# Convolution matrices read in four row groups without their zero columns, and another order of the first loads

## The chip, the cores and the metric

The kernel runs on one core of one Trainium2 chip. The metric is the device time of one execution in microseconds (us), lower is better. Four runs of the kernel before gave 3228.2 to 3229.64 us, with a median of 3228.65.

## The reference

Two layers work on `x` of shape (32, 384, 28, 28) in float32: a ConvNeXt block, and a channel gate on its output. Cut to what matters:

```
# layer 0
y = depthwise 7x7 convolution of x (padding 3) + dw_b
y = layer norm of y over the 384 channels, times ln_g, plus ln_b
y = gelu(y @ w1 + b1)                       # 384 -> 1536
y = grn_g * (y * nx) + grn_b + y            # nx: norm over positions / mean of the norms
x = x + (y @ w2 + b2)                       # 1536 -> 384
# layer 1
avg, max, min of x over positions -> small products (W1, W2_1, W2_2, W3, Wfc) -> logits
out = sigmoid(logits[:, :, None, None] + x)
```

## The kernel before

The kernel has two stages: first the depthwise convolution of all 32 images, then, image by image, norm, first product, gelu, second product and gate. The change is in the first stage and in the loads ahead of it.

**The convolution as matrix products.** An image of 28 by 28 is cut into seven strips of four rows, and each row is padded to 32 columns, so a strip of one channel is 128 values: one partition each. For each channel, the 49 weights become a banded matrix that takes a strip to a strip. Three products per channel (L309, L310, L313) take a strip to itself and to its two neighbours, with 224, 192 and 192 columns (strips times images).

The matrices of one channel are one table row. `tab` (128 channels by 3 blocks by 448 columns) is cleared, the 49 weights are copied into it with a row distance of 32 (L183), and the three blocks are stored to `fs` in DRAM (L187). `load_t(s)` reads from `fs` the matrices of the eight channels of step `s` into `tmat[s % 3]`: the same row is read by each of the 128 partitions, one element later in each, so that the shifted copies form the matrix. One read covers 128 partitions by 8 channels by `MW` = 320 columns; most of the columns at the edges of the row are zeros from the cleared table. The first 32 columns of each `tmat` buffer are cleared once by POOL (L195).

**The turned x.** The products need x with strip positions on the partitions. `load_x(i)` (L227) reads 32 channels of four images as a tile `xi` (four buffers), `pad_x(i)` (L237, POOL) copies it into one of two `xpad` buffers with 32 columns per row, and `turn_x` (L248, L253) transposes the seven strips on TensorE and copies them from PSUM into `xt` by VectorE. Eight groups make one block of 32 channels, `xt`; there are 12 blocks.

**The loop.** 48 steps of eight channels: each issues `load_t(s + 2)`, does the 24 products, evacuates them with the bias `dwb` by ScalarE (L327) or VectorE (L319) into `yc`, and between the products pads and turns one group of the next block per four channels. Every second step stores `yc` to `yd` (L345). From step 4 on each step also has POOL form one combination of blocks of `w1s` or `w2s` (`form_w`, L270 and L272) and store it; 15 of each. These feed the second stage, which is a scheme with fewer products than the plain one.

**The order.** Tile's scheduler sets the order of the instructions of each engine and inserts the waits: it goes by the order in the program, but may let an instruction whose inputs it takes for ready pass others of its engine. On one engine, and on SP, which issues nearly all of the DMAs, instructions then run strictly in that order, so one that waits holds all behind it. The loads ahead of the loop stand in the program as:

```
nc.sync.dma_start(dww, ...); nc.sync.dma_start(cv, ...)      # L150, L154
... tab cleared and filled, fs stored; dwb loaded (L197)
for s in range(2): load_t(s)
for i in range(4): load_x(i)
nc.sync.dma_start(w1s, ...)                                  # L279
for i in range(NG): pad_x(i); load_x(i + 4); turn_x(i, 0..1)
nc.sync.dma_start(w2s, ...); nc.sync.dma_start(fv, ...)      # L287, L288
```

`cv` holds per-channel vectors for the second stage, `fv` those of the 1536 middle channels.

Of the kernel before, what the change touches and what calls it, by code (L numbers as in the profile page):

```python
# [13 lines left out]
P = 128  # L14
C = 384
CB = C // P
# [15 lines left out]
PW = P // RW  # L32
XC = 32
TC = 8
YC = 16
NB = P // XC
REACH = 3 * PW
MW = P + 2 * REACH
FL = MW + P
NLAST = XC // YC  # L40


# [71 lines left out]
def convnext_gate_kernel(  # L114
# [13 lines left out]
    nc = tc.nc  # L128
# [11 lines left out]

    fs = [dram.tile([P, FL], F32, name=f"fs_{cb}") for cb in range(CB)]
    NY = C // YC
    yd = dram.tile([P, NY - NLAST, B, NJ * YC], F32, name="yd")
    u1d = dram.tile([KT, P, NS, P], F32, name="u1d")
    u2d = dram.tile([NS, P, KT * P], F32, name="u2d")
    yl = dram.tile([P, NLAST, B, NJ * YC], F32, name="yl")


    dww = const.tile([P, CB, 49], F32, name="dww")
# [1 line left out]
    ident = const.tile([P, P], F32, name="ident")  # L151
    make_identity(nc, ident)
    cv = const.tile([P, 5, CB], F32, name="cv")
    nc.sync.dma_start(cv, cvec.rearrange("v (cb p) -> p v cb", p=P))  # L154
    _, lng_t, lnb_t, b2_t, w21_t = (cv[:, i, :] for i in range(5))
    fv = const.tile([P, 3, FB], F32, name="fv")
    b1_t, gg_t, gb_t = (fv[:, i, :] for i in range(3))
# [9 lines left out]
    with ExitStack() as one:  # L167
# [8 lines left out]
        w1s = tp.tile([P, CB, FF], F32, name="w1s")  # L176
        w2s = tp.tile([P, FB, C], F32, name="w2s")
        tab = tp.tile([P, CB, FL], F32, name="tab")
        nc.vector.memset(tab, 0.0)

        t0 = REACH + P - 1 - 3 * PW - 3
        for cb in range(CB):
            nc.vector.tensor_copy(  # L183
                tab[:, cb, t0 : t0 + 7 * PW].rearrange("p (y x) -> p y x", x=PW)[:, :, :7],
                dww[:, cb, :].rearrange("p (y x) -> p y x", x=7),
            )
            nc.sync.dma_start(fs[cb], tab[:, cb, :])  # L187

        NT2 = 3
        T0 = P - REACH
        tmat = [tp.tile([P, TC, T0 + MW], F32, name=f"tmat_{i}") for i in range(NT2)]
        for t in tmat:
            nc.gpsimd.memset(t[:, :, :T0], 0.0)  # L195
        dwb = tp.tile([P, C], F32, name="dwb")
        nc.sync.dma_start(dwb, cvec[0:1, :].broadcast_to([P, C]))  # L197
        NK = C // TC

        def load_t(s):  # L200
            base = fs[s * TC // P]
            c0 = s * TC % P
            nc.sync.dma_start(
                tmat[s % NT2][:, :, T0:],
                bass.AP(
                    tensor=base.tensor,
                    offset=base.offset + c0 * FL,
                    ap=[[1, P], [FL, TC], [1, MW]],
                ),
            )  # L210


        NPAD = 2
# [4 lines left out]
        NG = B // NB  # L218
# [3 lines left out]
        def load_x(i):  # L222

            k, g = divmod(i, NG)
            t = xis[i] = xip.tile([P, NT], F32, tag="xi", name=f"xi_{i}")
            base = x[g * NB, k * XC : k * XC + 1, :]
            nc.sync.dma_start(  # L227
                t,
                bass.AP(
                    tensor=base.tensor,  # L230
                    offset=base.offset,
                    ap=[[NT, XC], [C * NT, NB], [1, NT]],
                ),
            )

        def pad_x(i):
            nc.gpsimd.tensor_copy(  # L237
                xpad[i % NPAD][:, :, :HW], xis.pop(i).rearrange("p (r w) -> p r w", w=HW)
            )
# [18 lines left out]
        def new_xt(k):  # L258
            return xtp.tile([P, XC, N], F32, tag="xt", name=f"xt_{k}")
# [12 lines left out]
                    nc.gpsimd.tensor_tensor(t, t, blk, ALU.add if sg > 0 else ALU.subtract)  # L272
            nc.sync.dma_start(dst, t)

        for s in range(2):
            load_t(s)
        for i in range(4):
            load_x(i)
        nc.sync.dma_start(w1s, w1.rearrange("(cb p) f -> p cb f", p=P))  # L279
        xt = new_xt(0)  # L280
        for i in range(NG):
            pad_x(i)
            if i + 4 < GT:
                load_x(i + 4)
            for h in range(2):
                turn_x(i, h, xt)
        nc.sync.dma_start(w2s, w2.rearrange("(fb p) c -> p fb c", p=P))  # L287
        nc.sync.dma_start(fv, fvec.rearrange("v (fb p) -> p v fb", p=P))  # L288
        SK = XC // TC
        GS = NG // SK  # L290
        for s in range(NK):
            k, si = divmod(s, SK)
            if s + 2 < NK:
                load_t(s + 2)
            if si == 0:
                xn = new_xt(k + 1) if k + 1 < NX else None
            if s % 2 == 0:
                kt = s // 2
                yc = ycp.tile([P, B, NJ, YC], F32, tag="yc", name=f"yc_{kt}")
            if s == NK - 2:  # L300
                warm = smp.tile([P, 1], F32, tag="warm", name="warm", bufs=1)
                nc.scalar.activation(warm, eps_t, AF.Sqrt)
            t = tmat[s % NT2]
            for c2 in range(TC // 2):
                pc = psc.tile([P, 2, 256], F32, tag="pc", name=f"pc_{s}_{c2}")
                for ci in range(2):
                    c = 2 * c2 + ci
                    xc = xt[:, si * TC + c, :]
                    nc.tensor.matmul(pc[:, ci, :N], t[:, c, P : 2 * P], xc, start=True, stop=False)  # L309
                    nc.tensor.matmul(  # L310
                        pc[:REACH, ci, : N - B], t[:, c, 2 * P :], xc[:, B:], start=False, stop=False
                    )
                    nc.tensor.matmul(  # L313
                        pc[:, ci, B:N], t[:, c, :P], xc[:, : N - B], start=False, stop=True
                    )
                cc = s * TC + 2 * c2
                cy = cc % YC
                if c2 % 2:
                    nc.vector.tensor_tensor(  # L319
                        yc[:, :, :, cy : cy + 2].rearrange("p b j c -> p c j b"),  # L320
                        pc[:, :, :N].rearrange("p c (j b) -> p c j b", j=NJ),
                        dwb[:, cc : cc + 2].unsqueeze(2).unsqueeze(3).to_broadcast([P, 2, NJ, B]),
                        ALU.add,
                    )
                else:
                    for ci in range(2):
                        nc.scalar.activation(  # L327
                            yc[:, :, :, cy + ci].rearrange("p b j -> p j b"),
                            pc[:, ci, :N].rearrange("p (j b) -> p j b", j=NJ),
                            AF.Identity,  # L330
                            bias=dwb[:, cc + ci : cc + ci + 1],
                            scale=1.0,
                        )
                if xn is not None:
                    g, h = divmod(si * (TC // 2) + c2, 2)
                    i = (k + 1) * NG + g
                    if h == 0:
                        pad_x(i)
                        if i + 4 < GT:
                            load_x(i + 4)  # L340
                    turn_x(i, h, xn)
            if s % 2:
                yv = yc.rearrange("p b j c -> p b (j c)")
                if kt < NY - NLAST:
                    nc.sync.dma_start(yd[:, kt], yv)  # L345
                else:
                    i = kt - (NY - NLAST)
                    for j in range(NJ):
                        nc.vector.bn_stats(bs0[:, j, 1 + i, :], yc[:, 0, j, :])
                    nc.vector.tensor_copy(yis[0][:, kt], yc[:, 0])  # L350
                    nc.sync.dma_start(yl[:, i], yv)
                if kt == NY - NLAST - 1:

                    yi = yis[0] = yip.tile([P, NY, NJ, YC], F32, tag="yi", name="yi_0")
                    nc.sync.dma_start(
                        yi[:, : NY - NLAST].rearrange("p k j c -> p k (j c)"), yd[:, :, 0, :]
                    )
                    bs0 = smp.tile([P, NJ, 1 + NLAST, 6], F32, tag="bs0", name="bs0", bufs=1)
                    for j in range(NJ):
                        nc.vector.bn_stats(bs0[:, j, 0, :], yi[:, : NY - NLAST, j, :])  # L360
            if si == SK - 1:
                xt = xn
            i = s // 2 - 2
            if 0 <= i < NS:
                if s % 2 == 0:
                    form_w(f"u1_{i}", w1v, UPSTEPS[i][1], u1d[:, :, i, :].rearrange("t p c -> p t c"))
                else:
                    form_w(
                        f"u2_{i}", w2v, STEPS[i][1], u2d[i].rearrange("p (t c) -> p t c", c=P)
                    )  # L370
# [470 lines left out]
```

## Time and profile before

| | |
|---|---|
| median of 4 runs | 3228.65 us |
| profiled execution, own time | 3230.04 us |
| its span (first to last instruction) | 3228.2 us |
| TensorE (PE) busy | 3177.5 us, 98% |
| first convolution product | 37.33 us from the start |
| last matrix load issued | 485.1 us |
| DMA traffic | 534.10 MB, mean 165 GB/s |

The profile is of one execution. Engines: PE is TensorE's products, PEld its weight loads, DVE VectorE, ACT ScalarE, POOL GpSimd, and SPq the queue of SyncE, which issues DMAs. L203 is line 203 of the kernel before. A timeline row gives the start and the length in us, the engine, the line, the operation, what it writes and reads, shapes and count, and in brackets the idle time of the engine ahead of it with what ended it. A row of waits gives the total in us, the number of times and the longest. "x" after a number in a row of stretches is the count of instructions; the last columns are TensorE's granted clock, the mean busy share of the 16 DMA engines, and GB/s.

### The profile page before, as it was taken

The numbers are of one execution on the slowest core, as the hardware profiler recorded it, in microseconds if no ns is written. First come the engines' busy times: TensorE is split into PE (matmuls) and PEld (weight loads), VectorE is DVE, ScalarE is ACT, GpSimd is POOL, SyncE is SP. The second block draws the span as 40 slices with busy tenths as digits, with TensorE's granted clock in tenths as the row PEclk, the third lists the DMA queues.
The fourth block names the chain that finished last, engine by engine and source line by source line (L and its number), as shares of the span: only waits on it lengthen the run. The fifth ranks groups of instructions, "written<-read, shape, count | busy, mean of one in ns | idle before, by whom it ended". The sixth has DMA issues, their size and how long they took to land.

```text
span 3228.2 us, 35684 instructions
## 1 busy us (share of the span) xinstructions
PE 3177.5 (98%) x12352; PEld 2012.4 (62%) x12352; DVE 1676.2 (52%) x3447; ACT 1882.0 (58%) x3024; POOL 1604.8 (50%) x813
## 2 busy tenths in 40 slices
PE   7999998999999999999999999999999999999998
PEld 6999996555555555555555555555555555555555
DVE  3443336555555555555555555555555555555553
ACT  1222224866666666666666666666666666666662
POOL 2455311555555555555555555555555555555555
PEclk9999999999999999999999999999999999999999
DMA  9999986434444444444444444444444444444333
GB/s 305 339 334 331 315 285 213 129 112 142 141 142 139 135 132 140 142 132 142 145 134 143 145 134 144 134 143 145 145 131 137 131 134 143 140 142 141 123 104 125
DMA packets 300150, 534.10 MB, mean 165 GB/s; under 512 B 121004, under 2 KB 179908, under 8 KB 296900
## 3 DMA queue, kind: packets, MB, share of 16 engines
q1 hardware_dynamic: 287572, 494.51, 47.1%
q10 hardware_dynamic: 12400, 37.33, 3.4%
q8 instruction: 98, 1.61, 0.2%
q14 instruction: 80, 0.66, 0.1%
HBM read 440.65 MB, written 91.13 MB: 165 GB/s over the span
## 4 chain that ended last, share of the span: by engine, by line
PE 87%; ACT 1%; DVE 1%; issue 0%; ACTq 0%; DVEq 0%
PE ph_A L549 13%; PE ph_B L549 13%; PE pz_A L646 11%; PE pz_B L646 10%; PE pz_C L646 5%; PE pz_E L646 5%; PE ph_C L549 5%; PE pz_F L646 3%; PE pz_G L646 3%; PE pz_D L646 3%; PE ph_H L549 3%; PE ph_D L549 3%; PE ph_F L549 3%; PE py L475 2%; PE pc L309 2%; PE pc L310 1%
## 5 line engine op out<-in xcount | busy, mean ns | idle before, releaser
L621 POOL TENSOR_TENSOR d_v<-d_u,y 128x1568 f32<-128x1568 f32 x32 | 112.4, 3511 | 759.6 <-PE pz_B L646 735.5
L524 ACT ACTIVATE y<-y,fv 128x784 f32<-128x784 f32 x384 | 346.8, 941 | 214.6 <-DVE y L564 214.0
L457 ACT ACTIVATE y<-y,fv,gsc 128x784 f32<-128x784 f32 x378 | 358.6, 1027 | 29.8 <-DVE gsc L591 29.8
L327 ACT ACTIVATE yc<-pc,dwb 128x224 f32<-128x224 f32 x192 | 103.7, 641 | 402.8 <-PE pc L313 303.5
L530 ACT ACTIVATE junk<-y 128x784 f32<-128x784 f32 x384 | 326.7, 851 | 5.0
L621 POOL TENSOR_TENSOR d_p<-y 128x1568 f32<-128x1568 f32 x31 | 109.0, 3518 | 434.6 <-ACT y L457 434.6
L549 PE MATMUL ph_A<-af,u 128*128 128x392 f32 x768 | 313.4, 502 | 5.5 <-DVE af L515 5.4
L549 PE MATMUL ph_B<-af,u 128*128 128x392 f32 x768 | 311.3, 493 | 0.3 <-ACT y L556 0.3
L646 PE MATMUL pz_A<-y,u 128*128 128x392 f32 x768 | 268.8, 493 | 0.0
L621 POOL TENSOR_TENSOR y<-d_v,y 128x1568 f32<-128x1568 f32 x64 | 223.5, 3513 | 2.5
L549 PEld LDWEIGHTS ph_A<-af,u 128*128 128x128 f32 x768 | 136.1, 190 | 135.1 <-ACT y L556 57.6
L549 PE MATMUL ph_A<-acc,u 128*128 128x392 f32 x512 | 216.3, 504 | 0.0
L309 PE MATMUL pc<-xt,tmat 128*128 128x224 f32 x768 | 209.3, 354 | 4.9 <-issue 4.9
L549 PE MATMUL ph_B<-acc,u 128*128 128x392 f32 x512 | 213.6, 499 | 0.1
L549 PEld LDWEIGHTS ph_B<-af,u 128*128 128x128 f32 x768 | 145.1, 190 | 108.9 <-DVE y L560 9.6
L646 PEld LDWEIGHTS pz_A<-y,u 128*128 128x128 f32 x768 | 145.8, 190 | 106.4
L556 ACT ACTIVATE y<-ph_A 128x392 f32<-128x392 f32 x256 | 124.7, 487 | 144.9 <-PE ph_A L549 144.8
L560 DVE TENSOR_TENSOR y<-y,ph_A 128x392 f32<-128x392 f32 x128 | 72.0, 562 | 237.9 <-PE ph_A L549 224.6
L446 ACT ACTIVATE sd<-mv,eps_t 128x7 f32<-128x7 f32 x32 | 9.6, 300 | 314.3 <-DVE mv L441 314.3
L515 POOL TENSOR_TENSOR af<-af,acc 128x392 f32<-128x392 f32 x186 | 186.9, 1017 | 4.9
L310 PE MATMUL pc<-xt,tmat 128*96 128x192 f32 x768 | 187.6, 326 | 0.0
L313 PE MATMUL pc<-xt,tmat 128*128 128x192 f32 x768 | 187.6, 326 | 0.0
(153 smaller groups left out, 6907.1 us busy)
## 6 DMA issues: line engine op xcount, KB each, us to landing
u<-u1d SPq DMA_DIRECT2D x128, 960.0 KB, 4.6
u<-u2d SPq DMA_DIRECT2D x480, 256.0 KB, 2.7
tmat<-fs SPq DMA_DIRECT2D x48, 1280.0 KB, 7.8
yd<-yc SPq DMA_DIRECT2D x22, 1792.0 KB, 11.3
yi<-yd SPq DMA_DIRECT2D x32, 1232.0 KB, 6.9
xi<-in_x SPq DMA_DIRECT2D x96, 392.0 KB, 8.5
x<-in_x SPq DMA_DIRECT2D x32, 1176.0 KB, 5.8
out<-x ACTq DMA_DIRECT2D x31, 1176.0 KB, 5.0
```

Source lines behind the costliest of these rows:

```text
L309: nc.tensor.matmul(pc[:, ci, :N], t[:, c, P : 2 * P], xc, start=True, stop=False)
L310: nc.tensor.matmul(pc[:REACH, ci, : N - B], t[:, c, 2 * P :], xc[:, B:], start=False, stop=False)
L313: nc.tensor.matmul(pc[:, ci, B:N], t[:, c, :P], xc[:, : N - B], start=False, stop=True)
L327: nc.scalar.activation(yc[:, :, :, cy + ci].rearrange("p b j -> p j b"), pc[:, ci, :N].rearrange("p (j b) -> p j b", j=NJ), AF.Identity, b ...
L457: eng.activation(out, in_, AF.Identity, bias=add, scale=mul)
L515: eng.tensor_tensor(d, o[in0], o[in1], op)
L524: nc.scalar.activation(y, y, AF.Gelu, bias=b1_t[:, f : f + 1], scale=1.0)
L530: nc.scalar.activation(junk, ys[b][:, f, :], AF.Square, accum_out=ssqs[b][:, f : f + 1])
L549: nc.tensor.matmul(banks[bk][:, :NH], wt[:, i, :], o[opnd], start=(first == 1), stop=True, skip_group_check=True,)
L556: nc.scalar.activation(d, p, AF.Identity)
L621: nc.gpsimd.tensor_tensor(d, o[in0], o[in1], op)
L646: nc.tensor.matmul(pz[:, :NH], wt[:, t, :], o[opnd][:, t, :], start=(first == 1 and t == 0), stop=(t == KT - 1), skip_group_check=True,)
```

## The change

1. `load_t` reads each buffer in four DMAs of 32 partitions (`GR` = 32) instead of one of 128. Group `g` (0, 32, 64, 96) leaves out columns that are zero in all its 32 partitions: it reads 227, 230, 230 and 227 columns for the four groups, instead of 320.
2. The three `tmat` buffers are cleared whole on VectorE, instead of 32 columns of each on POOL; the first of them between the clearing of `tab` and the copies into it, the others after these.
3. The stores of `fs` are issued on ScalarE's queue instead of SP's.
4. The first four x loads stand ahead of `load_t(0)`; `dwb` and `load_t(1)` come at the fifth pad.
5. `w1s`, `w2s`, `fv` and `cv` are loaded at steps 2, 3, 4 and 5 of the loop. Ahead of each load, POOL copies one column of `yc` into the tile that is to be loaded, so the load waits for a product of the loop.

```diff
+S0 = REACH + P - 1 - 3 * PW - 3
+S1 = S0 + 6 * PW + 7
+GR = 32
...
-    nc.sync.dma_start(cv, cvec.rearrange("v (cb p) -> p v cb", p=P))
...
-        nc.vector.memset(tab, 0.0)
-        t0 = REACH + P - 1 - 3 * PW - 3
-        for cb in range(CB):
-            nc.vector.tensor_copy(tab[:, cb, t0 : ...], dww[:, cb, :]...)
-            nc.sync.dma_start(fs[cb], tab[:, cb, :])
...
-        for t in tmat:
-            nc.gpsimd.memset(t[:, :, :T0], 0.0)
         dwb = tp.tile([P, C], F32, name="dwb")
-        nc.sync.dma_start(dwb, cvec[0:1, :].broadcast_to([P, C]))
+        nc.vector.memset(tab, 0.0)
+        nc.vector.memset(tmat[0], 0.0)
+        for cb in range(CB):
+            nc.vector.tensor_copy(tab[:, cb, S0 : ...], dww[:, cb, :]...)
+            nc.scalar.dma_start(fs[cb], tab[:, cb, :])
+        for t in tmat[1:]:
+            nc.vector.memset(t, 0.0)
...
         def load_t(s):
             base = fs[s * TC // P]
             c0 = s * TC % P
-            nc.sync.dma_start(
-                tmat[s % NT2][:, :, T0:],
-                bass.AP(tensor=base.tensor, offset=base.offset + c0 * FL,
-                        ap=[[1, P], [FL, TC], [1, MW]]),
-            )
+            for g in range(0, P, GR):
+                m0, m1 = max(0, S0 - g - GR + 1), min(MW, S1 - g)
+                nc.sync.dma_start(
+                    tmat[s % NT2][g : g + GR, :, T0 + m0 : T0 + m1],
+                    bass.AP(tensor=base.tensor, offset=base.offset + c0 * FL + g + m0,
+                            ap=[[1, GR], [FL, TC], [1, m1 - m0]]),
+                )
...
-        for s in range(2):
-            load_t(s)
         for i in range(4):
             load_x(i)
-        nc.sync.dma_start(w1s, ...)
+        load_t(0)
         xt = new_xt(0)
         for i in range(NG):
             pad_x(i)
+            if i == NG - 4:
+                nc.sync.dma_start(dwb, cvec[0:1, :].broadcast_to([P, C]))
+                load_t(1)
             if i + 4 < GT:
                 load_x(i + 4)
             for h in range(2):
                 turn_x(i, h, xt)
-        nc.sync.dma_start(w2s, ...)
-        nc.sync.dma_start(fv, ...)
+        later = {2: (w1s, ...), 3: (w2s, ...), 4: (fv, ...), 5: (cv, ...)}
...
             if s + 2 < NK:
                 load_t(s + 2)
+            if s in later:
+                dst, src = later[s]
+                nc.gpsimd.tensor_copy(dst[:, 0, :1], yc[:, 0, 0, :1])
+                nc.sync.dma_start(dst, src)
```

More of the change, by code (lines that the diff above doesn't have):

```diff
@@ L178, in convnext_gate_kernel @@
         tab = tp.tile([P, CB, FL], F32, name="tab")
-        nc.vector.memset(tab, 0.0)
-        t0 = REACH + P - 1 - 3 * PW - 3
-        for cb in range(CB):
-            nc.vector.tensor_copy(
-                tab[:, cb, t0 : t0 + 7 * PW].rearrange("p (y x) -> p y x", x=PW)[:, :, :7],
-                dww[:, cb, :].rearrange("p (y x) -> p y x", x=7),
-            )
-            nc.sync.dma_start(fs[cb], tab[:, cb, :])
         NT2 = 3
@@ L193, in convnext_gate_kernel @@
         tmat = [tp.tile([P, TC, T0 + MW], F32, name=f"tmat_{i}") for i in range(NT2)]
-        for t in tmat:
-            nc.gpsimd.memset(t[:, :, :T0], 0.0)
         dwb = tp.tile([P, C], F32, name="dwb")
-        nc.sync.dma_start(dwb, cvec[0:1, :].broadcast_to([P, C]))
+        nc.vector.memset(tab, 0.0)
+        nc.vector.memset(tmat[0], 0.0)
+        for cb in range(CB):
+            nc.vector.tensor_copy(
+                tab[:, cb, S0 : S0 + 7 * PW].rearrange("p (y x) -> p y x", x=PW)[:, :, :7],
+                dww[:, cb, :].rearrange("p (y x) -> p y x", x=7),
+            )
+            nc.scalar.dma_start(fs[cb], tab[:, cb, :])
+        for t in tmat[1:]:
+            nc.vector.memset(t, 0.0)
         NK = C // TC
@@ L202, in load_t @@
             c0 = s * TC % P
-            nc.sync.dma_start(
-                tmat[s % NT2][:, :, T0:],
[L205 to L210, printed above, removed]
+            for g in range(0, P, GR):
+                m0, m1 = max(0, S0 - g - GR + 1), min(MW, S1 - g)
+                nc.sync.dma_start(
+                    tmat[s % NT2][g : g + GR, :, T0 + m0 : T0 + m1],
+                    bass.AP(
+                        tensor=base.tensor,
+                        offset=base.offset + c0 * FL + g + m0,
+                        ap=[[1, GR], [FL, TC], [1, m1 - m0]],
+                    ),
+                )
         NPAD = 2
@@ L273, in form_w @@
             nc.sync.dma_start(dst, t)
-        for s in range(2):
-            load_t(s)
         for i in range(4):
             load_x(i)
-        nc.sync.dma_start(w1s, w1.rearrange("(cb p) f -> p cb f", p=P))
+        load_t(0)
         xt = new_xt(0)
@@ L286, in convnext_gate_kernel @@
                 turn_x(i, h, xt)
-        nc.sync.dma_start(w2s, w2.rearrange("(fb p) c -> p fb c", p=P))
-        nc.sync.dma_start(fv, fvec.rearrange("v (fb p) -> p v fb", p=P))
+        later = {
+            2: (w1s, w1.rearrange("(cb p) f -> p cb f", p=P)),
+            3: (w2s, w2.rearrange("(fb p) c -> p fb c", p=P)),
+            4: (fv, fvec.rearrange("v (fb p) -> p v fb", p=P)),
+            5: (cv, cvec.rearrange("v (cb p) -> p v cb", p=P)),
+        }
         SK = XC // TC
```

## The prediction

> **What bounds the kernel now.** I read the busy shares first, then the start in stretches of 2 us and as a timeline, then what TensorE waited for during the convolution, then stretches of 20 us, then the DMA issues. The page says who is the bound:
>
> ```profile
> PE 3177.5 (98%) x12352; PEld 2012.4 (62%) x12352; DVE 1676.2 (52%) x3447; ACT 1882.0 (58%) x3024; POOL 1604.8 (50%) x813
> ```
>
> TensorE is idle for 50.7 us of 3228.2 in all. The change touches only the start and the convolution (0 to 510 us), so its gain is capped by the idle time there. The timeline of the start:
>
> ```profile
> 8.03 0.84 POOL L237 COPY xpad<-xi 128x784 f32<-128x784 f32 x1 [5.53 <-DMA xi<-in_x]
> 8.62 1.00 SPq L203 DMA_DIRECT2D tmat<-fs  x2
> 9.66 4.43 SPq L227 DMA_DIRECT2D xi<-in_x  x2
> ...
> 21.55 0.84 POOL L237 COPY xpad<-xi 128x784 f32<-128x784 f32 x1 [10.02 <-DMA xi<-in_x]
> ...
> 28.16 1.49 POOL L270 TENSOR_SCALAR u<-w1s 128x512 f32<-128x512 f32 x1 [4.76 <-DMA w1s<-in_w]
> ...
> 30.49 6.93 PE L248 MATMUL pt<-ident,xpad 128*128 128x128 f32 x35 [4.79 <-POOL xpad L237]
> ...
> 37.33 0.65 PE L309 MATMUL pc<-xt,tmat 128*128 128x224 f32 x2
> ```
>
> The first product starts at 37.33. It needs eight x loads, padded by POOL and turned by TensorE. Loads 2 and 3 stand behind two matrix loads on SP, so POOL waits 10.02 us. Then POOL waits for w1s, since a product with w1s (written at step 4) was ordered ahead of pads 4 to 7. TensorE does 63 turns (nine groups of seven, one of them of the next block) in 13.7 us, so it is idle for 23.6 us before 37.33. This is the stall that the change can reach. During the convolution TensorE waits for little (waits of PE, 37 to 512 us):
>
> ```profile
> PE pc L309 <- issue: 4.9, 11, 1.1
> PE pt L248 <- POOL xpad L237: 1.9, 2, 1.5
> PE pt L248 <- DVE xt L253: 0.4, 1, 0.4
> ```
>
> But the DMA engines are as full as TensorE (columns: PE, PEld, DVE, ACT, POOL busy, clock, DMA share, GB/s):
>
> ```profile
> 4.00:6.00 2.00, 0.00 (x0) 0.00 (x0) 0.00 (x0) 0.00 (x0) 0.00 (x0) 1.00 0.94 114
> 6.00:8.00 2.00, 0.00 (x0) 0.00 (x0) 0.00 (x0) 0.00 (x0) 0.00 (x0) 1.00 0.98 375
> ...
> 100.00:120.00 20.00, 19.62 (x126) 18.87 (x125) 8.44 (x13) 4.17 (x8) 7.08 (x8) 1.00 0.99 344
> ...
> 340.00:360.00 20.00, 18.09 (x115) 17.11 (x115) 8.29 (x13) 3.23 (x6) 11.67 (x11) 1.00 0.94 318
> ```
>
> ```profile
> u<-u2d SPq DMA_DIRECT2D x480, 256.0 KB, 2.7
> tmat<-fs SPq DMA_DIRECT2D x48, 1280.0 KB, 7.8
> ...
> w1s<-in_w SPq DMA_DIRECT2D x1, 2304.0 KB, 13.9
> ```
>
> **The change part by part.** *The head of SP's queue.* cv leaves it (0.48 us of issue, and 1920 items of 4 bytes, beside which the engines were 94% busy at 114 GB/s between 4 and 6 us), dwb moves behind x, and the three fs stores go to ACT's queue, where nothing waits behind them. x0 to x3 are then issued from about 1.3 us at 0.55 each, instead of at 2.83, 5.18, 9.66 and 13.49. x0 took 5.2 us to its pad beside cv and dwb, so it lands by 6.5, and 0.40 MB at the 375 GB/s of the next row is 1.07 us more for each: x3 by 9.7.
>
> *VectorE.* The table's memset (1344 columns, 1.18 us) is followed by one of 2816 columns, 2.47 us at the same rate, ahead of the three copies (0.42 us). They end at 1.14 + 1.18 + 2.47 + 0.42 = 5.2 instead of 3.4. The first fs store goes out at about 4.95 and lands 5.0 us later (its own row): 9.95. Two further memsets of 2.47 us keep VectorE until 10.1, and behind them wait the copies of turned x, whose first came at 10.07 before; three PSUM buffers hold TensorE up after a group and a half. x4 covers this, landing later than 15; without that cover it would cost 2 to 3 us. POOL loses 0.81 us of memsets: nothing.
>
> *Load 0.* Four issues of 0.37 to 0.58 us instead of one: 10.0 to 11.8. A whole load landed after 6.2 us at the least: 16.2. x4 to x7 are issued behind it (their slots are free once pads 0 to 3 are through, by about 11) and stream at 1.07 us each: x7 at 20.5. From the start of a pad to the second copy's end the first group took 3.3 us (8.03 to 11.27). **First product at 23.8**, I take 24.0. If x4 to x7 get ahead of load 0, it is 20.5; if fs lands 4 us later, 28. Shift 13.3 us. One group of seven turns (1.5 us) that was done ahead of 37.33 will stand inside the convolution: **11.8 us** net. With the pads back to back, TensorE's own eight groups would have allowed 17 to 18; the DMA engines are what is late next.
>
> *w1s, w2s, fv, cv at steps 2 to 5.* 4.7 MB, and 6528 items of 4 bytes, now go beside the convolution; before, only w2s and fv did. Each waits on SP for a small POOL copy, which waits for ScalarE's first output of a pair of steps. Behind the copy on POOL are pads; behind the load on SP are x and matrix loads. The copy itself is one column (the smallest POOL row is 0.10 us). Before, POOL stood 9.0 us for w2s and SP 10.38 us in one matrix load's issue right behind fv, and TensorE lost 1.9 us to xpad. Two big loads at that price are about 4 us; w1s comes where little else is due, so I take 2.5. Bounds 0 and 12: two waits of 9.0 us less one pad period of 4.9 us that the second xpad buffer covers give 8.2, and 4 more for two stalls of SP.
>
> *The clock.* It read 0.50 between 30 and 36 us, after TensorE's idle 25.7 to 30.5, and fell on turns. TensorE will now idle from about 14 to 17. Should half clock reach the first products, 6.8 us of it cost at most 3.4. I take 0.5.
>
> *The matrices.* The groups read 227, 230, 230 and 227 columns instead of 320: 0.936 MB for 1.311 MB, but the same 1024 rows. In 1280 KB per load, 392 per x, 1792 per yd and 256 per form, two steps moved 6.59 MB in 19.7 us, 334 GB/s, and will move 5.84 MB, 297 GB/s. TensorE sets the pace of these steps, so fewer bytes bring nothing there by themselves; the 4.9 us of "issue" stay (bounds: minus 4.9 to 0). SP gets 144 more issues, 1.1 to 1.5 us per step of 9.85, in which it now spends some 2.5 us issuing. The price of a load split by rows is in no row of the trace. At 340 GB/s one load takes 3.86 us; by bytes the new one takes 2.75, by rows the same 3.86, and four unoverlapped transfers of 256 KB (2.7 us each to landing) would be 10.8. I take 2.75 to 3.86, since landings overlap everywhere in this trace (48 loads of 7.8 us fit among the others), and so no cost: the DMA share of about 0.97 leaves 0.6 us per two steps.
>
> [...]
>
> **Sum.** -11.8 + 2.5 + 0.5 = -8.8. The profiled execution took 3230.04 us (span 3228.2 and 1.84 around it), 1.4 above the median of 3228.65. So 3221.2 for a profiled one, **3219.9 for the median**. With the bounds of the start (20.5 to 28) and the usual part of the stalls, this case runs from 3214 to 3224.
>
> **The rivals.** *The DMA engines become the bound (slower).* For it: the share near 1 in every stretch up to 360 us, and row counts that do not fall. Against it: 29% fewer bytes. It decides once a load takes over 3.86 + 0.3 = 4.2 us; above, each us costs two per pair of steps, 24 pairs. At 5.0 us: (2 x 1.14 - 0.6) x 24 = 40 us, less 8.8: 3260; at 4.5 us it is 3234.
>
> *The late weights take the place of the stall (no change).* POOL stands for w1s and w2s with pads behind, 12 us as bounded: 11.8 gained and 12 to 13 lost, about 3229. For it: forms were put ahead of pads twice before (4.8 and 9.0 us). Against it: only 1.9 us reached TensorE.
>
> *It does not do what it says.* The instruction order is made by a scheduler with its own clock; if it puts load 0 or 1, with its wait for fs, ahead of most x loads, the first product comes at about 32: 5.3 - 1.5 = 3.8 us, less some stall, 3226.
>
> **How the numbers follow.** Main case 0.60, DMA bound 0.15, late weights 0.17, order 0.08. About 0.2% (6.5 us) is what a measurement can tell from no change. Faster by more: 0.58 of the main case and 0.04 from the milder ends of the next two, 0.62. Slower by more: 0.14 of the DMA case and 0.03 of the late weights, 0.17. Same: 0.21. The range 3213 to 3236 takes in the main case, both cases of no change and the mild end of the DMA case; some 0.15 stays out.
>
> **What would show it.** Right: first product between 20 and 28 us; POOL's 10.02 us wait and the w1s wait before it gone; DMA share in the 100 to 360 us stretches near 0.85 with about 297 GB/s; waits of PE on xpad within a few us. Wrong: a DMA share still near 1 at below 300 GB/s with waits of the products on tmat (DMA bound); POOL forms waiting 8 us or more for w1s or w2s and TensorE for xpad (late weights); matrix loads ahead of x2 to x5 on SP (order). A longer stretch after the convolution would be outside all of this.

## The result and the profile after

| | before | after |
|---|---|---|
| median | 3229.35 us (46 runs) | 3237.32 us (28 runs, 3233.14 to 3242.25) |
| ratio | 1 | 1.0024 [1.0019, 1.0029] |
| profiled execution, own time / span | 3230.04 / 3228.2 us | 3234.73 / 3232.7 us |
| first product | 37.33 us | 26.68 us |
| first product to the end of the last one of the convolution | 472.42 us | 488.10 us |
| from there to the end | 2718.5 us | 2717.9 us |

The change makes the kernel 8 us slower. The profiled execution of after is one of the quicker ones, 2.6 us under its median. Its three stretches say where to look: the start gained 10.65 us, the convolution lost 15.7, and behind it next to nothing changed (0.5 us). TensorE still carries the span:

```profile
PE 3180.1 (98%) x12352; PEld 2018.1 (62%) x12352; DVE 1680.0 (52%) x3450; ACT 1881.7 (58%) x3024; POOL 1606.4 (50%) x814
```

The start, from the timeline of after:

```profile
5.22 0.84 POOL L240 COPY xpad<-xi 128x784 f32<-128x784 f32 x1 [3.47 <-DMA xi<-in_x]
5.35 1.84 ACTq L196 DMA_DIRECT2D fs<-tab  x3
...
11.02 1.81 SPq L206 DMA_DIRECT2D tmat<-fs  x4
...
12.94 2.48 SPq L230 DMA_DIRECT2D xi<-in_x  x4
...
19.02 0.84 POOL L240 COPY xpad<-xi 128x784 f32<-128x784 f32 x1 [5.14 <-DMA xi<-in_x]
...
26.68 0.64 PE L323 MATMUL pc<-xt,tmat 128*128 128x224 f32 x2 [0.92 <-DVE xt L256]
```

The first pad comes at 5.22 instead of 8.03, the waits of 10.02 us for x and of 4.76 us for w1s are gone, and what is late now is x4, whose issue stood behind load 0 (12.94) and whose pad waits until 19.02. From there TensorE's turns set the pace, 1.42 us from pad to pad on the mean. The waits of PE in the convolution (37 to 512 us) of after:

```profile
PE pc L323 <- issue: 11.1, 10, 1.1
PE pc L323 <- DMA tmat<-fs: 7.1, 4, 3.8
PE pt L251 <- POOL xpad L240: 0.4, 1, 0.4
```

Two things are new: the "issue" waits, 4.9 us in 11 before, are 11.1 in 10, and products wait 7.1 us for matrix loads. The wait for pads, which the prediction feared, fell from 1.9 to 0.4. The stretches of 20 us of after (columns as before: PE, PEld, DVE, ACT, POOL, clock, DMA share, GB/s):

```profile
80.00:100.00 20.00, 16.11 (x84) 14.69 (x83) 5.72 (x9) 2.38 (x5) 8.15 (x8) 0.83 1.07 224
100.00:120.00 20.00, 17.72 (x112) 16.72 (x111) 7.45 (x15) 4.31 (x8) 6.40 (x8) 1.00 1.00 274
...
340.00:360.00 20.00, 18.88 (x121) 18.11 (x120) 8.08 (x12) 4.35 (x8) 14.32 (x13) 1.00 1.06 285
```

Fewer bytes per second than before, 285 against 318, and yet a share of 1.06 against 0.94: the loads are smaller and yet keep the engines longer. (The share adds up the times of all packets, so it can pass 1.) The stall in the first of these stretches, from the timeline of after; first SP's queue, then one x load of its last row and TensorE:

```profile
62.89 1.58 SPq L308 DMA_DIRECT2D w2s<-in_w  x1
65.87 6.53 SPq L230 DMA_DIRECT2D xi<-in_x  x2
...
73.39 3.78 SPq L206 DMA_DIRECT2D tmat<-fs  x4
79.36 3.12 SPq L308 DMA_DIRECT2D fv<-in_fvec  x1
82.57 9.09 SPq L230 DMA_DIRECT2D xi<-in_x  x2
...
92.39 2.22 SPq L206 DMA_DIRECT2D tmat<-fs  x4
```

```profile
82.57 8.44 SPq L230 DMA_DIRECT2D xi<-in_x  x1
...
90.71 0.71 PE L323 MATMUL pc<-xt,tmat 128*128 128x224 f32 x1 [3.85 <-DMA tmat<-fs]
```

The matrices that come 3.85 us late are those of step 6. Their buffer was free from the end of step 3, at 65.7 us, but SP stood in the issues of x loads behind `w2s`, so their four transfers went out at 73.39 to 77.17 and landed 13.5 to 14.1 us after their issue. After that SP issues `fv`, 4608 items of 4 bytes, and then stands 8.44 us in the issue of one x load; this holds the next matrices (92.39), not those of step 6. The granted clock of the stretch is 0.83 where it was 1.00 in the rest of the convolution.

### The profile page after: what moved, and what is told of

Same layout as the page of the kernel before. It is cut to its first block, busy times and chain, and to the rows that moved or that the text cites. A ratio compares the mean times of both kernels' runs of the same rounds, so it can differ in the third digit from the quotient of the medians.

```text
span 3232.7 us, 35931 instructions
## 1 busy us (share of the span) xinstructions
PE 3180.1 (98%) x12352; PEld 2018.1 (62%) x12352; DVE 1680.0 (52%) x3450; ACT 1881.7 (58%) x3024; POOL 1606.4 (50%) x814
## 4 chain that ended last, share of the span: by engine, by line
PE 95%; DMA 2%; DVE 1%; ACT 1%; issue 1%; SPq 0%; ACTq 0%; DVEq 0%
PE ph_A L563 14%; PE ph_B L563 13%; PE pz_A L660 11%; PE pz_B L660 10%; PE pz_C L660 5%; PE ph_C L563 5%; PE pz_E L660 5%; PE pc L323 4%; PE pc L324 3%; PE pc L327 3%; PE pz_F L660 3%; PE ph_D L563 3%; PE ph_F L563 3%; PE ph_H L563 3%; PE pz_G L660 3%; PE pz_D L660 3%
## 5 line engine op out<-in xcount | busy, mean ns | idle before, releaser
L323 PE MATMUL pc<-xt,tmat 128*128 128x224 f32 x768 | 211.0, 357 | 19.1 <-issue 11.1
L256 DVE COPY xt<-pt 128x512 f32<-128x512 f32 x192 | 117.0, 616 | 152.6 <-PE pt L251 152.6
L240 POOL COPY xpad<-xi 128x784 f32<-128x784 f32 x96 | 80.3, 839 | 230.2 <-PE pt L251 114.5
```

The source lines that it names most:

```text
L256: nc.vector.tensor_copy(xv[:, j0:j1, :, g * NB : (g + 1) * NB], pt[:, : j1 - j0, :].rearrange("p j (c q) -> p j c q", q=NB),)
```

## The experiments

All differences below are the ratio less one times 3229.4 us, because the medians of before moved a little between the three sets of runs (e, f and h: 3229.45, 3229.78, 3231.17), each from another chip. The diffs are against after, except where it says otherwise.

| kernel | matrices | weights | turns at a block's end | ratio [95%] | against before |
|---|---|---|---|---|---|
| after | 4 x 32 neighbouring rows | late | as scheduled | 1.0024 [1.0019, 1.0029] | +7.8 |
| e1_whole | one, 320 columns | late | as scheduled | 0.9963 [0.9951, 0.9976] | -11.9 |
| e2_split | as after | as before, start too | as scheduled | 1.0019 [1.001, 1.0028] | +6.1 |
| e3_dealt | 4 x every 4th row, 230 | late | as scheduled | 0.9984 [0.9976, 0.9993] | -5.2 |
| f3_rows230 | 4 x 32 neighbouring, 230 | late | as scheduled | 1.0025 [1.0015, 1.0034] | +8.1 |
| e4_early | as after | early | as scheduled | 1.0005 [0.9996, 1.0014] | +1.6 |
| f1_ahead | as after | late | ahead | 1.0007 [0.9998, 1.0016] | +2.3 |
| f2_whole_ahead | one, 320 | late | ahead | 0.9947 [0.9934, 0.9959] | -17.1 |
| f4_one230 | one, 230 | late | as scheduled | 1.0037 [1.0024, 1.005] | +11.9 |
| h1_dealt_ahead | 4 x every 4th row, 230 | late | ahead | 0.9957 [0.9944, 0.9969] | -13.9 |
| h2_early_ahead | as after | early | ahead | 0.9972 [0.9961, 0.9982] | -9.0 |
| h3_whole_early_ahead | one, 320 | early | ahead | 0.9957 [0.9943, 0.997] | -13.9 |
| h4_one230_pinned | one, 230 | late | as scheduled, forms held | 0.9958 [0.9945, 0.997] | -13.6 |

My theory after the result: the start does what it should, and the split of the matrix loads by rows costs all of it and more. The rival: the late weights stall the stage, whatever the matrices look like.

### The new start without the split (e1_whole)

```diff
-            for g in range(0, P, GR): ...   # four DMAs
+            nc.sync.dma_start(tmat[s % NT2][:, :, T0:],
+                bass.AP(tensor=base.tensor, offset=base.offset + c0 * FL,
+                        ap=[[1, P], [FL, TC], [1, MW]]))
```

> The changed kernel with each conv load as one transfer of 128 rows by 320 columns again; all else of the change stays. Theory A (the split into four transfers of 32 rows fills the DMA engines, and the convolution pays for it): the first product stays at about 26 to 27 us, the waits of the products on tmat go (7.1 us before this edit), the ten waits of TensorE on nothing shown fall back from 1.1 to about 0.4 us each, and the time is about 3222, 7 us below the kernel before. Theory B (the late loads of w1s, w2s, fv and cv cost what the start gained): the stall of 3.9 us at 87 us stays and the time is 3230 or more. If 1.31 MB instead of 0.94 MB per load hurts by itself, tmat waits grow instead.

3218.06 us, 11.9 under before and 19.7 under after. First product at 25.87. Waits of PE (37 to 512 us) of e1_whole:

```profile
PE pc L321 <- issue: 5.3, 10, 1.1
...
PE pc L321 <- DMA tmat<-fs: 1.2, 1, 1.2
```

So the late weights are not what the change loses by themselves: they are in this kernel, and it is the faster one. Both new waits go with the split. The load for step 6 is issued at 66.34 here; it takes 15.3 us to land, and nothing waits for it.

### The split without the new start (e2_split)

```diff
 # before, with
-        for t in tmat: nc.gpsimd.memset(t[:, :, :T0], 0.0)
+        for t in tmat: nc.vector.memset(t, 0.0)
 # and the four DMAs of load_t
```

> The kernel before with the split loads alone (four transfers of 32 rows, the tmat buffers cleared whole on VectorE); w1s, w2s, fv, cv, dwb and the order of the loads as before. Theory A: the first product at 37 to 39 us, DMA share near 1.07 at about 300 GB/s in the convolution, waits of TensorE of 1.1 us ten times, and 3237 to 3242, 8 to 13 us above the kernel before. Theory B: the split is free, 3227 to 3231.

3235.84 us, 6.1 over before, between the two ranges that were expected; first product at 37.33 as before. Its "issue" waits are 12.2 us in 11, its waits on `tmat` 0.8 in one. The split alone thus costs 6 us, all of the size of the new "issue" waits (7.3 more than before), and less than the 19.7 that it costs together with the new start. Something in the new start makes it dearer.

### The weights early again (e4_early)

```diff
+    nc.sync.dma_start(cv, ...)               # at its old place
...
         load_t(0)
+        nc.sync.dma_start(w1s, ...)
...                                           # behind the first block
+        nc.sync.dma_start(w2s, ...); nc.sync.dma_start(fv, ...)
-        later = {...}                         # and the loads at steps 2 to 5
```

> The changed kernel with w1s loaded right behind the first conv load, w2s and fv behind the first block, and cv first of all, as in the kernel before; the split of the conv loads stays. Theory A: the start is worse (first product 30 to 34 us), the convolution keeps its waits of 1.1 us, 3238 or more. Theory B: the stall at 87 us goes with its half clock (about 7 us), the start loses 4 to 8, and the time is 3232 to 3237.

3230.89 us, 6.1 under after and under both expected ranges, although the first product comes at 30.7, 4 us later. The waits on `tmat` fall from 7.1 to 1.6 us and the stretch of 80 to 100 us runs at clock 1.00; the "issue" waits stay (12.2). The dearer part is the late weights, but only with split loads, since e1_whole has them too.

### The same four transfers with other rows (e3_dealt, f3_rows230)

Both read 230 fixed columns in four DMAs of 32 rows: the same bytes, sizes and number. Only which rows go together differs: rows g, g+4, g+8, ... or 32 neighbours. The fixed window leaves out part of the weights in many rows, so these two kernels, and the other ones with 230 columns below, do not compute the reference's result; their products, bytes and transfers are as described.

```diff
 # e3_dealt
-                m0, m1 = max(0, S0 - g - GR + 1), min(MW, S1 - g)
+                m0, m1 = 45, 275
-                    tmat[s % NT2][g : g + GR, :, ...]    # ap=[[1, GR], ...]
+                    tmat[s % NT2][g::4, :, ...]          # g in 0..3, ap=[[4, GR], ...]
 # f3_rows230: the line of m0, m1 alone
```

> The changed kernel with the rows of a load dealt to its four transfers in steps of four (transfer g takes rows g, g+4, g+8 and so on) in place of 32 neighbouring rows; every row reads the same window of 230 columns, so parts of the convolution's bands are left out. Number, size and order of the transfers are those of the change. [...] Theory A2 (four transfers cost more than one by their number): as the change, 3234 to 3240, DMA share 1.07.

> The changed kernel, each of the four transfers with its 32 neighbouring rows but with the same window of 230 columns in every row (parts of the bands are left out): the control of the kernel with dealt rows, from which it differs only in which rows go together. [...] Theory A2 (the number of transfers) or the window itself: as the kernel with dealt rows, 3223 to 3226.

3224.65 and 3237.52 us: a difference of 13.2 us by the ratios, from the choice of rows alone; f3_rows230 equals after. The stretch of 240 to 280 us, first of e3_dealt, then of f3_rows230:

```profile
240.00:280.00 40.00, 38.89 (x248) 37.52 (x247) 15.71 (x25) 8.69 (x16) 15.97 (x15) 1.00 0.84 289
```

```profile
240.00:280.00 40.00, 38.90 (x248) 37.50 (x247) 16.07 (x24) 8.70 (x16) 16.44 (x15) 1.00 1.08 291
```

At the same 290 GB/s the DMA engines are 84% busy in one and 108% in the other. The DMA issues say the same, again e3_dealt and then f3_rows230 (count, KB each, median us to landing):

```profile
tmat<-fs SPq DMA_DIRECT2D x192, 230.0 KB, 6.5
```

```profile
tmat<-fs SPq DMA_DIRECT2D x192, 230.0 KB, 10.1
```

TensorE waits 0.6 us for `tmat` in e3_dealt and 7.2 in f3_rows230, and f3_rows230 has the clock of 0.83 between 80 and 100 us. The longest of the waits of f3_rows230 is again that of step 6: its load goes out at 72.44 in f3_rows230 and at 68.66 in e3_dealt, where SP stands 4.09 us in the x loads ahead of it instead of 6.54, and its landing takes 14.0 and 13.4 us. The "issue" waits are 11.1 in both, so these have nothing to do with the rows. The two profiled spans are only 7.7 us apart (3223.7 and 3231.4): that of f3_rows230 is from the quickest of its ten runs, that of e3_dealt from the slowest of its eleven. What the other runs of f3_rows230 wait for is not seen in a profile.

### The "issue" waits (f1_ahead, f2_whole_ahead)

The end of a block of 32 channels in the timeline of after:

```profile
65.51 0.49 PE L251 MATMUL pt<-ident,xpad 128*128 128x128 f32 x3
65.71 0.91 DVE L333 TENSOR_TENSOR yc<-pc,dwb 128x448 f32<-128x448 f32 x1 [1.37 <-PE pc L327]
66.47 0.53 DVE L256 COPY xt<-pt 128x384 f32<-128x384 f32 x1
67.10 0.62 PE L323 MATMUL pc<-xt,tmat 128*128 128x224 f32 x2 [1.10 <-issue]
```

The same place in the timeline of before:

```profile
75.40 1.25 PE L248 MATMUL pt<-ident,xpad 128*128 128x128 f32 x10
75.60 0.96 DVE L319 TENSOR_TENSOR yc<-pc,dwb 128x448 f32<-128x448 f32 x1 [1.37 <-PE pc L313]
76.40 1.60 DVE L253 COPY xt<-pt 128x384 f32<-128x384 f32 x3
77.04 0.62 PE L309 MATMUL pc<-xt,tmat 128*128 128x224 f32 x2 [0.39 <-issue]
```

The product at 67.10 needs the last turned strips of its block. Their copy (66.47) stands on VectorE behind a bias add of 0.91 us, so TensorE waits 1.10 us, and the label "issue" hides that. Before, the scheduler's order has seven more turns in that place, of the block after (10 instead of 3), and they fill most of the wait: 0.39 us is left. With whole loads (e1_whole) they are there at eight of ten block ends; at the block ends with a wait of 1.1 us in after, e2_split, e3_dealt, e4_early and f3_rows230, three turns stand there. The two kernels below do the last three turns of a block ahead of the four products that end it, so that their copy is in time:

```diff
             for c2 in range(TC // 2):
+                ahead = xn is not None and si == SK - 1 and c2 == TC // 2 - 1
+                if ahead:
+                    turn_x((k + 1) * NG + NG - 1, 1, xn)
...
-                if xn is not None:
+                if xn is not None and not ahead:
```

> The changed kernel with one edit: at the last four channels of each block the last three turns of the next block stand ahead of the products, not behind them, so the last copy into xt is done while TensorE multiplies. Theory C (the waits of 1.1 us that the profile gives to nothing are waits at the end of each block for VectorE's copy into xt, which stands behind a bias addition of 0.9 us; they were 0.38 us before because the scheduler put seven more turns there, and with the split loads it no longer does): the ten waits go, and the time is 3224 to 3228, 9 to 11 us below the change. If they are instruction fetches that the fuller DMA engines delay, they stay at 1.1 us and the time stays at 3234 to 3240.

> The changed kernel with whole conv loads of 128 rows by 320 columns and the last three turns of a block ahead of its last products. Theory C: the 5.3 us of such waits go too, 3212 to 3214, 15 us below the kernel before. If they are fetches: 3217 to 3219 as with whole loads alone.

3231.22 us, 5.5 under after, a miss (3224 to 3228 were expected), and 3212.65, 5.2 under e1_whole. The "issue" waits are gone from both. Waits of PE of f1_ahead (37 to 512 us), then of f2_whole_ahead (0 to 520 us):

```profile
PE pc L326 <- DMA tmat<-fs: 11.2, 6, 5.0
PE pt L251 <- POOL xpad L240: 2.8, 4, 1.1
```

```profile
PE pc L324 <- DMA tmat<-fs: 2.2, 1, 2.2
```

In f1_ahead more than half of the 11.1 us came back as longer waits, for matrices (7.1 to 11.2 us) and for pads (0.4 to 2.8). f2_whole_ahead, the new start with whole loads, is the quickest of all.

### Fewer bytes in one transfer (f4_one230, h4_one230_pinned)

```diff
 # f4_one230
-            for g in range(0, P, GR): ...
+            nc.sync.dma_start(tmat[s % NT2][:, :, T0 + 45 : T0 + 275],
+                bass.AP(..., offset=base.offset + c0 * FL + 45,
+                        ap=[[1, P], [FL, TC], [1, 230]]))
 # h4_one230_pinned: besides, ahead of each form of w1s and w2s
+            nc.gpsimd.tensor_copy(t[:, 0, :1], yc[:, 0, 0, :1])
```

> The changed kernel with one transfer per conv load, 128 rows by the same window of 230 columns (parts of the bands are left out): the bytes of the change in one transfer. If fewer bytes are worth nothing while TensorE sets the pace: 3216 to 3219, as with whole loads of 320 columns, at a DMA share of about 0.8 instead of 0.93. If the DMA engines still held the whole loads up: 3212 to 3215.

f4_one230 was a miss: 3242.08 us, 11.9 over before. Its matrices are never waited for; its pads are. Waits of PE (37 to 512 us) and, from POOL's timeline, the reason:

```profile
PE pt L249 <- POOL xpad L238: 18.2, 9, 4.5
PE pc L321 <- issue: 4.5, 10, 1.1
```

```profile
238.89 1.49 POOL L271 TENSOR_SCALAR u<-w1s 128x512 f32<-128x512 f32 x1 [6.95 <-DMA u1d<-u]
240.47 1.26 POOL L273 TENSOR_TENSOR u<-u,w1s 128x512 f32<-128x512 f32 x1
241.70 1.49 POOL L271 TENSOR_SCALAR u<-w2s 128x512 f32<-128x512 f32 x1
243.15 3.95 POOL L273 TENSOR_TENSOR u<-u,w1s 128x512 f32<-128x512 f32 x3
```

The scheduler ordered the forms of the weights earlier (the last one begins by 286 us, against 356 in e1_whole), so POOL stands in a form whose buffer is still being stored, with pads behind it. h4_one230_pinned holds each form back with a copy of one column that waits for the step's own output:

> One transfer of 128 rows by 230 columns per conv load (parts of the bands are left out), with a small POOL copy from yc ahead of each form, so that no form can run before its own steps. Theory D (the 3242 of this load without the copy came from forms that the scheduler put some 15 steps ahead, between the pads, where POOL waited for them): TensorE's waits on xpad after the start go (19 us) and the time is 3216 to 3220, as with whole loads of 320 columns (3218.06): 29% fewer bytes bring nothing. If a load of 920-byte rows is slow by itself: 3235 or more.

3217.92 us, within the interval of e1_whole (3218.06): 28% fewer bytes bring nothing, and f4_one230's 25 us were the order on POOL. Between 240 and 260 us h4_one230_pinned moves 308 GB/s at a DMA share of 0.90, e1_whole 329 at 0.93, TensorE at 20.00 of 20 us in both.

### All parts together (h1_dealt_ahead, h2_early_ahead, h3_whole_early_ahead)

These combine the edits above: e3_dealt, e4_early, and whole loads with early weights, each with the turns ahead.

> The changed kernel with dealt rows (four transfers per load, rows in steps of four, one window of 230 columns, so parts of the bands are left out) and the last turns of a block ahead of its last products. [...] If four transfers cost something by their number, 3218 or more.

> The changed kernel with the weights loaded early (as in the kernel before) and the last turns of a block ahead; loads split as in the change. [...]

> Whole conv loads, turns ahead, and w1s, w2s, fv and cv loaded early again; the new order of x, dwb and the conv loads stays. Against whole loads and turns ahead with late weights (3212.65): if the late loads are what makes the start short, 3216 to 3220 with a first product at 29 to 32 us; if they only move the load, 3211 to 3214.

3217.73, 3221.53 and 3217.14 us. With f1_ahead and f2_whole_ahead, the last two make a square in which only the loads and the place of the weights differ:

| against before | weights early | weights late | late less early |
|---|---|---|---|
| one load of 128 rows | -13.9 (h3) | -17.1 (f2) | -3.2 |
| four of 32 neighbouring rows | -9.0 (h2) | +2.3 (f1) | +11.3 |
| split less whole | +4.9 | +19.4 | |

Neither edit is dear by itself: the split costs 4.9 us and the late weights measure 3.2 less, which would make +1.7 in all. Together they cost 16.2 (from -13.9 to +2.3), 14.5 more. The intervals reach 3 to 4 us to either side, so the 3.2 may be nothing. For the 4.9 the intervals overlap too, though every run of h2 is slower than every run of h3. The 11.3, the 19.4 and the 14.5 are clear. The split also moves the weights, since the scheduler sets the order anew: `w1s` is issued at 51.76 us in after and at 37.48 in e1_whole. This is not the reason: in h1_dealt_ahead it is issued at 50.75. The same kernel shows that it is the rows and not the number of transfers: with late weights its four DMAs give -13.9. It is 5.1 us above f2_whole_ahead (3212.65); part of that is the higher level of its set (before 3231.17), and the rest, 3.2 us by the ratios, lies within the two intervals. Its profile has one wait of 3.4 us for `tmat`; whether four DMAs cost that as such is open.

## Why the prediction was wrong

It said 3219.9 us with a range of 3213 to 3236; it was 3237.32, on the other side of no change and 1.3 us outside the range.

**The start: right.** First product at 26.68 for 24.0, within 20 to 28. Of the late 2.7 us, 1.7 are x4, behind load 0 on SP as the working had it, but padded at 19.02 where it was to land by 17.3. The rest is the pace behind it: 1.07 us for each x load was the price of the DMA engines, but the pads came 1.42 us apart on the mean, those of the last two waiting for TensorE's turns (0.92 and 0.65 us). Together with the late loads the new start gave -11.9 with whole loads (e1_whole), where the sum had -8.8.

**The matrices: the step that failed.** The term was 0; split against whole loads it measured +19.7 us (after against e1_whole). Two parts of the working failed in it.

- "I take 2.75 to 3.86, since landings overlap everywhere in this trace": landings of whole loads do overlap (before, 48 of 7.8 us and 96 x loads of 8.5 us, both medians, were issued between 2.8 and 485.1 us), but a transfer of 32 neighbouring rows was in no row of the trace, and it takes longer without moving more (10.1 us to landing where the dealt rows take 6.5, 230 KB in both). This is 13.2 us (f3_rows230 against e3_dealt). My two ends for the price of a load were both made from transfers that covered 128 partitions. What should have told me is that the rival built on it had no evidence against it but the bytes, and bytes were shown there to be no limit (TensorE was busy for 19.62 of the 20 us from 100 on). Its profile sign, "a DMA share still near 1 at below 300 GB/s with waits of the products on tmat", is what came: 1.08 at 291 GB/s. Its size was nearer than the forecast (3234 at 4.5 us per load; its own formula gives 3236). But the engines did not become the bound at every step, as its formula had it: TensorE waited for `tmat` four times in all.
- "The 4.9 us of "issue" stay (bounds: minus 4.9 to 0)": they rose to 11.1, and no bound allowed a rise. I took the label at its word; it was TensorE waiting for a copy on VectorE, and what filled the wait were turns that the scheduler no longer put there. About 6 us: 5.8 by the waits of after against e1_whole, 6.8 by e3_dealt against e1_whole, 6.1 by e2_split against before.

**The late weights: a wrong sum, for a reason.** I priced them by themselves at +2.5. With whole loads they cost nothing (-3.2, within the intervals); with the split they cost 6.1 (after against e4_early) to 11.3 (f1_ahead against h2_early_ahead). Their way was not the one that I priced: pads that came late hardly reached TensorE (0.4 us). What reached it was SP's queue, which had a place in the bounds alone (4 us for two stalls): the four issues of the load for step 5 took 6.85 us from first to last (0.36 for the one issue in e1_whole; 1.1 to 1.5 more was forecast), w2s and x loads came behind them, and the load for step 6 went out 7 us later than in e1_whole. How much of its 13.5 to 14.1 us to landing, against a median of 9.9 in the whole kernel, is due to w2s, `fv` or the split is not separated. I had costed each part against a stage in which the other part was as before. The DMA share of about 0.97 left little room, and I gave it to each of them.

**The clock.** 0.5 us for half clock ahead of the first products; instead the stall at 86.86 to 90.71 us was followed by it (0.50 between 92 and 96 us). In the stretch of 80 to 100 us the mean clock was 0.83; 0.17 of 20 us is an estimated 3.4 us.

**The choice of rows.** The pair e3_dealt and f3_rows230 shows it: 0.84 against 1.08 of the engines' time for the same bytes, and 6.5 against 10.1 us to landing. The two kernels also read rows that lie 1 or 4 elements apart in DRAM; that the near ones are slow by themselves is unlikely, since h4_one230_pinned reads 128 rows 1 element apart in one DMA and moves 296 GB/s at a share of 0.89 in the same stretch (240 to 280 us). By what way 32 neighbouring rows keep the engines longer is not shown by any run.

**Still open.** Why the scheduler drops the seven turns with four DMAs per load, and what the runs of after that are longer than the profiled one wait for.

## What to carry to other kernels

When a transfer is cut by partitions, cost it by which partitions go together and not by bytes or rows (13.2 us here, at the same bytes and number of rows); where the trace has no transfer of that shape, the far end of its price is a real case. Two edits that use the same spare room (here the DMA engines, and SP's queue beside them) must be costed together, since each can be cheap alone (here +4.9 and -3.2 us, and +16.2 together). When a product waits for a load, look up when that load was issued: what stands in the queue behind it cannot be the reason for a late issue. And look up what a wait labelled "issue" really follows before you say that it stays: a look at the last copy on the other engine was enough.

## What the runs showed of the hardware

Rows dealt out in steps of four cut the landing time of a quarter load from 10.1 to 6.5 us at nearly the same total rate (289 and 291 GB/s). Right behind the issue of a load of 4608 items of 4 bytes, SP stood 8.44 us in its next issue (10.38 in the kernel before). One wait of TensorE of 3.85 us, in a stage that is busy otherwise, was followed by a granted clock of 0.83 over the 20 us around it; in f1_ahead, whose longest wait for matrices was 5.0 us, it was 0.91 over the same 80 to 100 us, with TensorE busy for 14.01 of the 20.
